# A Mamba scan on one core: the C rows stay in SBUF and only their changing half is refilled

## The chip, the core and the metric

The kernel runs on one core of a Trainium2 chip. A core has five engines that work side by side: TensorE (PE; PEld is its weight load), VectorE (DVE), ScalarE (ACT), GpSimd (POOL) and SyncE (SP), which here only issues DMAs. SBUF is the on-chip memory with 128 partitions, PSUM the matmul accumulator, and transfers are carried out by 16 DMA engines. The metric is the device time of one execution in microseconds (us).

## The reference

The input is x, [2, 96, 128, 128]. Layer 0 adds to x a four-direction Mamba over its normalised value, and then a quantised feed-forward; layer 1 adds a 3x3 convolution and a second feed-forward. The time lies in the Mamba. Each image has L = 16384 tokens, read in four orders: by rows, by rows backwards, by columns, by columns backwards. For each order (`xs4`, one set of weights each), with 192 channels d and 16 states s:

```python
xz = x @ in_w.T;  xc, z = jnp.split(xz, 2, axis=-1)
xc = jax.nn.silu(causal_conv4(xc) + conv_b)
xdbl = xc @ xproj_w.T                  # dt_raw (6), Bm (16), Cm (16) for each token
dt = jax.nn.softplus(dt_raw @ dt_w.T + dt_b)
def step(h, t):
    dA = jnp.exp(dt_t[:, :, None] * A)
    h = dA * h + dt_t[:, :, None] * B_t[:, None, :] * u_t[:, :, None]
    y = jnp.einsum('bds,bs->bd', h, C_t)
y = (ys + Dp * xc) * jax.nn.silu(z);   return y @ outp_w.T
```

B and C depend on the token and the state, not on the channel. So every channel (a partition of SBUF) needs the same row of B and of C, but each order has its own rows.

## The kernel before

For each of the two images there are three stages: `normalize` (layer norm, and a copy by columns to DRAM), `mamba`, and `ffn_and_conv`.

In `mamba` the two orders of a pair, rows and columns, go together: 2 x 192 channels fill three groups g of 128 partitions. Group 0 is the first order alone, group 2 the second alone, and group 1, the middle one, has the last 64 channels of the first and the first 64 of the second. A step is one pair and one stretch of T = 512 tokens; there are 2 pairs x 32 stretches for each image, 128 steps in all. Within a step the work goes over 24 units: the three groups, and in each the 16 states two by two (`units`, `nu`). Two units that follow one another are a quad of four states; a step has 12 quads.

For each unit ACT makes the decays `exp(dt * A)` into PSUM (`decay`), DVE runs two scans over 512 tokens (`scan`, L353), the state sequence h is multiplied with C (`behind`, L441, on DVE; in the six units of `BY_POOL` by POOL, L360), and PE adds the product into y by a matmul with the identity (`sums`, L357). Once in a quad POOL multiplies B with dt*u (`b_part`, L339), two units before the quad is scanned. When a group ends, DVE multiplies y with the gate (`gated`, L364) and PE projects it.

The rows of B and C come out of a matmul (`rows`), go to a DRAM tile `bcd` in the layout [B or C, quad, order, state, token], and are read back spread over 128 partitions by `row_tile` (L335): one 1 MB load for the B of a quad, into one of four buffers, and one for its C, into one of three. For groups 0 and 2 the source is one row of 8 KB repeated 128 times. For the middle group it is two rows, and the partitions alternate: even ones belong to the first order, odd ones to the second. The host lays the weights out in that order (`perm` in `_layout`). The middle group's conv and gate values come out of their matmul in halves (partitions 0 to 63 and 64 to 127), and are brought into the alternating order by DMAs (`mixed`, `mix`, L256).

The order of the work is written out by hand: each engine runs its instructions in program order (`in_order`), and `later`/`issue` put the next step's preparation (`prologue`) at given units. In iteration k of the main loop the calls are: the fetch of a B quad (k even), `feed` (POOL's multiplication for the quad after), the first scan of unit k, `behind(k - 1)` (product and sums of the unit before), the decays of unit k + 2, the second scan, the fetch of a C quad. A POOL product is issued at the end of the iteration after its unit's scans, and its sums two iterations later. All loads stand in SP's queue in this order, and a load waits there until the last reader of its buffer's former content is done.

Of the kernel before, what the change touches and what calls it, by code (L numbers as in the profile page):

```python
# [10 lines left out]
F32 = mybir.dt.float32  # L11
# [3 lines left out]
AF = mybir.ActivationFunctionType  # L15
ALU = mybir.AluOpType
# [13 lines left out]
HID = 384  # L30
PAIRS = ((0, 2), (1, 3))
NG = 3
B_AHEAD = 3
C_AHEAD = 2
AHEAD = 2
BY_POOL = tuple((g, s) for g in range(3) for s in (0, 8))
BCO = 32
NBC = 4 * S

# [2 lines left out]
def tile_metaformer(ctx: ExitStack, tc: tile.TileContext, a: dict, out: bass.AP):  # L42
# [142 lines left out]
    def mamba(acc, xnr, xnc):  # L185

        with ExitStack() as st:
            pool = lambda n, bufs, **kw: st.enter_context(tc.tile_pool(name=n, bufs=bufs, **kw))

            io, gen, one, mixp, two = (pool(*p) for p in (("io", 2), ("gen", 4), ("one", 1), ("mixp", 1), ("two", 2)))  # L190
# [23 lines left out]
            def prologue(pi, i, d):  # L214
# [34 lines left out]
                def mixed(name):  # L249
                    d["mix", name] = mixp.tile([128, T], F32, name="mix")  # L250
                    return d["mix", name]

                def mix(name):
# [51 lines left out]


                first = pi == 0 and i == 0
                at = [(-3, 1, load), (3, 0, partial(mix, "xc")), (11, 0, partial(silu, "xc"))]
                at += [(9, 0, partial(mix, "sz")), (31, 1, partial(silu, "sz"))]
# [28 lines left out]
            def b_part(i, d, g, s, b):  # L338
                nc.gpsimd.tensor_tensor(b, d["dtu"][g][:, None, :].broadcast_to((128, 4, T)), b, ALU.mult)  # L339
# [17 lines left out]
                    nc.tensor.matmul(y, ident, c[:, j, :], start=False, stop=s + j == S - 1)  # L357
# [32 lines left out]
            def later(k, where, rank, f, *args):  # L390
                todo.setdefault((k, where), []).append((rank, partial(f, *args)))
# [20 lines left out]
            prepare(1)  # L412
            bs, cs, das, hs, quads = {}, {}, {}, {}, {}

            def fetch(k, n, ahead, m):
                if k < total:
                    t = row_tile(state[k // nu], *units[k % nu], n, ahead)
                    m[k], m[k + 1] = t[:, 0:2, :], t[:, 2:4, :]
                    if n == 0:
                        quads[k] = t  # L420

            def feed(k):

# [11 lines left out]
            def behind(k):  # L435

                n, u = divmod(k, nu)
                (pi, i), d, (g, s) = steps[n], state[n], units[u]
                h, c = hs.pop(k), cs.pop(k)
                if (g, s) not in BY_POOL:  # L440
                    nc.vector.tensor_tensor(c, h, c, ALU.mult)  # L441
                nc.scalar.copy(hst[:, g, s : s + 2], h[:, :, T - 1])  # L442
                if s == 0:
                    if k > 0:
                        pn, pu = divmod(k - 1, nu)
                        gated(steps[pn][0], state[pn], units[pu][0], ys.pop(k - 1))
                    y = ps_y.tile([128, T], F32, name="y")
                    nc.tensor.matmul(y, dmat[:, pi, g, :], d["xc"][:, g, :], start=True, stop=False)  # L448
                else:
                    y = ys.pop(k - 1)  # L450
                ys[k] = y
                if (g, s) in BY_POOL:
                    later(k + 1, 1, True, by_pool, h, c)
                    later(k + 3, 1, True, sums, s, y, c)
                else:
                    sums(s, y, c)
# [6 lines left out]
            for m, (n, ahead) in ((bs, (0, B_AHEAD)), (cs, (1, C_AHEAD))):  # L463
                for k in range(ahead):
                    fetch(2 * k, n, ahead, m)
            feed(0)
            for k in range(AHEAD):
                feed_decay(k)
            for k in range(total + 6):
                n, u = divmod(k, nu)  # L470
                if u == nu - 3:

                    prepare(n + 2)
                if k % 2 == 0:
                    fetch(k + 2 * B_AHEAD, 0, B_AHEAD, bs)
                    feed(k + AHEAD)
                issue(k, 0)
                if k < total:
                    (g, s) = units[u]
                    da, b = das.pop(k), bs.pop(k)  # L480
                    hs[k] = b if (g, s) in BY_POOL else da
# [118 lines left out]
def _layout(v):  # L600

    f = np.float32
    order = [d for pair in PAIRS for d in pair]

    perm = np.arange(2 * DI)
    perm[128:256] = perm[128:256].reshape(2, 64).T.reshape(-1)
    grouped = lambda w: w.reshape(2, NG, 128, -1).transpose(2, 0, 1, 3)
    plain = lambda w: grouped(w[order].reshape(2, 2 * DI, -1))
    rows = lambda w: grouped(w[order].reshape(2, 2 * DI, -1)[:, perm])
# [19 lines left out]
    out = {  # L629
        "x": v["x"].reshape(NB, C, L),  # L630
        "ident": np.eye(128, dtype=f),
        "inx": v["L0_conv_in_w"][:, :DI].transpose(2, 0, 1),
        "inz": v["L0_conv_in_w"][:, DI:].transpose(2, 0, 1),
        "taps": v["L0_conv_conv_w"].transpose(0, 2, 1)[None],
        "convb": plain(v["L0_conv_conv_b"])[..., 0],
        "bcw": grouped(bcw[:, perm]),
        "dtw": dtw[:, :, perm],
        "dtb": rows(v["L0_conv_dt_b"])[..., 0],
        "alog": rows(v["L0_conv_A_log"]),
        "dskip": rows(v["L0_conv_Dp"])[..., 0],  # L640
        "outx": outx,
        "fusew": v["L0_conv_fuse_w"].reshape(C, 4, C).transpose(2, 1, 0),
        "fuseb": v["L0_conv_fuse_b"].reshape(C, 1),
        "kw": v["L1_conv_kernel"].transpose(1, 2, 3, 0).reshape(C, 9, C),
    }
# [23 lines left out]
```

## Time and profile before

| | us |
|---|---|
| median of 3 runs | 11550.38 (11546.19 to 11551.36) |
| profiled execution | 11556.77, its span 11555.0 |
| DVE busy | 10421.6 (90%) |
| PE busy | 10435.0 (90%) |
| POOL busy | 9672.3 (84%) |
| ACT busy | 7901.7 (68%) |
| DMA traffic | 3417 MB, 296 GB/s over the span |
| granted TensorE clock | 0.989 |

The two scan stages run from about 120 to 5200 us and from about 5900 to 10980 us. In the page's slices they are where DVE, PE and POOL show nines and the DMA engines eights; between and after them stand `ffn_and_conv` and `normalize`, with hardly any transfers. In a group's line the numbers after the bar are the busy time, the mean of one instruction in ns, and the idle time of the engine just before such an instruction with what ended most of it. In a line of waits they are the total in us, how often, and the longest.

### The profile page before, as it was taken

The page shows a single profiled execution, that of the slowest core. Times are in us where ns is not written, and L with a number is a line of the kernel's source. Part 1 is how long each engine was busy: PE and PEld are TensorE (multiplying, and loading weights), DVE is VectorE, ACT ScalarE, POOL GpSimd, SP SyncE. Part 2 cuts the span into 40 slices and gives each one's busy share as a digit, 9 for nine tenths or more (in the row PEclk, how much of TensorE's full clock was granted, in tenths as well). Part 3 has the DMA queues.
Part 4 walks back from the last instruction along what each step waited for, and adds up shares of the span by engine and source line. Part 5 has one row for each costly group of instructions (what it writes and reads, how often), then busy time and mean ns, then how long its engine had stood idle before and what let it go on. Part 6 is the DMA issues. An engine that isn't in the chain of part 4 may idle for free. (4 is left out here: it accounts for less than half of the span.)

```text
span 11555.0 us, 94102 instructions
## 1 busy us (share of the span) xinstructions
PE 10435.0 (90%) x24208; PEld 3971.4 (34%) x24208; DVE 10421.6 (90%) x10127; ACT 7901.7 (68%) x13564; POOL 9672.3 (84%) x4700
## 2 busy tenths in 40 slices
PE   7999999999999999989989999999999999999899
PEld 2333333333333333333323333333333333333333
DVE  6999999999999999994469999999999999999944
ACT  6767767677677677665567677677676776776655
POOL 5999999999999999991159999999999999999911
PEclk8999999999999999999989999999999999999999
DMA  7888888888888888880068888888888888888800
GB/s 263 335 329 333 333 332 332 330 331 333 329 332 333 330 331 333 329 322 19 26 243 334 328 331 334 330 333 333 333 331 329 332 332 329 331 333 329 319 13 13
DMA packets 540755, 3416.96 MB, mean 296 GB/s; under 512 B 67532, under 2 KB 68652, under 8 KB 143832
## 3 DMA queue, kind: packets, MB, share of 16 engines
q1 hardware_dynamic: 539960, 3410.16, 76.8%
q8 instruction: 196, 3.21, 0.1%
q14 instruction: 343, 2.81, 0.1%
q0 software_dynamic: 256, 0.79, 0.0%
HBM read 3289.04 MB, written 54.53 MB: 289 GB/s over the span
## 5 line engine op out<-in xcount | busy, mean ns | idle before, releaser
L339 POOL TENSOR_TENSOR row<-dtu,row 128x2048 f32<-128x2048 f32 x1536 | 6948.9, 4524 | 283.3 <-DMA row<-bcd 281.6
L357 PE MATMUL y<-row,ident 128*128 128x512 f32 x12288 | 5690.6, 603 | 700.0 <-DVE row L441 699.9
L353 DVE TENSOR_TENSOR_SCAN da<-da,row 128x512 f32<-128x512 f32 x4608 | 5456.9, 1214 | 38.9 <-ACT da L349 5.2
L349 ACT ACTIVATE da<-dt,amat 128x512 f32<-128x512 f32 x6144 | 4246.9, 691 | 170.2
L357 PEld LDWEIGHTS y<-row,ident 128*128 128x128 f32 x12288 | 2256.8, 190 | 4008.4 <-issue 2243.5
L441 DVE TENSOR_TENSOR row<-da,row 128x1024 f32<-128x1024 f32 x2304 | 2776.7, 1205 | 70.2 <-DMA row<-bcd 70.0
L442 ACT COPY hst<-da 128x2 f32<-128x2 f32 x2304 | 368.9, 160 | 2652.2 <-DVE row L441 2649.3
L360 POOL TENSOR_TENSOR row<-row,row 128x1024 f32<-128x1024 f32 x768 | 1807.4, 2353 | 223.0 <-DVE row L353 147.5
L353 DVE TENSOR_TENSOR_SCAN row<-da,row 128x512 f32<-128x512 f32 x1536 | 1852.4, 1206 | 91.9 <-POOL row L339 84.1
L211 PE MATMUL misc<-xa,inx 96*64 96x512 f32 (+1 forms) x2048 | 946.1, 605 | 50.0 <-ACT mix L239 26.8
L211 PE MATMUL misc<-xb,inx 96*64 96x512 f32 (+1 forms) x2048 | 952.3, 608 | 33.6 <-ACT hst L442 24.2
L564 POOL TENSOR_TENSOR acc<-acc,y 96x512 f32<-96x512 f32 x128 | 147.4, 1151 | 991.5 <-DVE y L563 991.5
L298 POOL TENSOR_TENSOR dtu<-dt,xc 128x512 f32<-128x512 f32 x384 | 487.4, 1269 | 106.0 <-DMA xb<-xnc 99.8
L576 PE MATMUL pc<-pad,kw 96*96 96x512 f32 x1152 | 566.4, 593 | 0.0
L211 PEld LDWEIGHTS misc<-xa,inx 96*64 96x64 f32 (+1 forms) x2048 | 327.3, 165 | 581.2 <-issue 438.0
L448 PE MATMUL y<-xc,dmat 128*128 128x512 f32 x768 | 419.5, 628 | 103.6 <-DVE sz L364 103.6
L374 PE MATMUL misc<-sz,gmat 128*96 128x512 f32 x1024 | 484.1, 595 | 0.0
L284 PE MATMUL misc<-rows,dtw 12*128 12x512 f32 x768 | 434.3, 645 | 50.6 <-ACT dt L289 37.9
L364 DVE TENSOR_TENSOR sz<-y,sz 128x512 f32<-128x512 f32 x384 | 264.6, 689 | 229.5 <-PE y L357 198.0
L136 DVE TENSOR_TENSOR xq<-xm,rs 96x512 fp8e5<-96x512 f32 x128 | 87.9, 687 | 392.2 <-ACT rs L132 392.2
L211 PEld LDWEIGHTS misc<-xb,inx 96*64 96x64 f32 (+1 forms) x2048 | 316.5, 164 | 361.9 <-issue 214.1
L372 PE MATMUL misc<-acc,ident 96*96 96x512 f32 x512 | 387.6, 842 | 57.3 <-ACT sz L247 53.8
(76 smaller groups left out, 7449.9 us busy)
## 6 DMA issues: line engine op xcount, KB each, us to landing
row<-bcd SPq DMA_DIRECT2D x3072, 1024.0 KB, 7.4
xc<-mix SPq DMA_DIRECT2D x256, 128.0 KB, 5.4
sz<-mix SPq DMA_DIRECT2D x256, 128.0 KB, 8.9
xa<-xnr SPq DMA_DIRECT2D x124, 193.1 KB, 8.6
xb<-xnc SPq DMA_DIRECT2D x124, 193.1 KB, 8.7
bcd<-rows SPq DMA_DIRECT2D x128, 128.0 KB, 9.5
acc<-in_x_dram SPq DMA_DIRECT2D x16, 768.0 KB, 5.7
xnr<-xn SPq DMA_DIRECT2D x16, 768.0 KB, 4.3
```

The source lines that it names most:

```text
L211: nc.tensor.matmul(ps[rows, :], w(PAIRS[pi][d], k, lo, hi), src[d][:, k : k + T], **se)
L284: nc.tensor.matmul(d["ps"], w, d["rows"][0 : 2 * RK, :], start=True, stop=True)
L298: nc.gpsimd.tensor_tensor(dtu, d["dt"][:, g, :], d["xc"][:, g, :], ALU.mult)
L339: nc.gpsimd.tensor_tensor(b, d["dtu"][g][:, None, :].broadcast_to((128, 4, T)), b, ALU.mult)
L349: nc.scalar.activation(da[:, j, :], d["dt"][:, g, :], AF.Exp, scale=amat[:, pi, g, s + j : s + j + 1])
L353: nc.vector.tensor_tensor_scan(h[:, j, :], da[:, j, :], b[:, j, :], 0.0, ALU.mult, ALU.add)
L357: nc.tensor.matmul(y, ident, c[:, j, :], start=False, stop=s + j == S - 1)
L360: nc.gpsimd.tensor_tensor(c, h, c, ALU.mult)
L374: nc.tensor.matmul(d["po"], gmat[:, pi, 2 * g - 2 + k, :], d["yg"][g - 1 + k], start=False, stop=k == 1)
L441: nc.vector.tensor_tensor(c, h, c, ALU.mult)
L448: nc.tensor.matmul(y, dmat[:, pi, g, :], d["xc"][:, g, :], start=True, stop=False)
L576: nc.tensor.matmul(pc, kw[:, t, :], rows, start=t == 0, stop=t == 8)
```

## The change

- The C rows are no longer loaded for each quad into rotating buffers. Four tiles `crow0` to `crow3`, one for each quad of states, stay for the whole stage. `c_fill` refills one of them when the products of its quad are done: from group 0 to group 1 only partitions 64 to 127 change their order of tokens, from group 1 to group 2 only partitions 0 to 63, and from group 2 to the next step's group 0 all 128.
- The middle group is in halves: partitions 0 to 63 belong to the first order, 64 to 127 to the second. So `perm`, `mixed` and `mix` go, and the source of the middle group's B load is written as two rows, each repeated 64 times (`src[:, None].broadcast_to((n, 128 // n, 4, T))`), where it was 64 repeats of two rows.
- The products with C are written into the unit's B buffer instead of the C buffer. There are five B buffers in place of four, `B_AHEAD` is 4 in place of 3, and the fetch stands after the second scan of the iteration, with the C fill behind it.
- POOL's products are those of the states s = 2 and 8 in each group, in place of 0 and 8.
- The program's scratch for DMAs issued by POOL is 4096 bytes.

```diff
-B_AHEAD = 3
-C_AHEAD = 2
+B_AHEAD = 4
-BY_POOL = tuple((g, s) for g in range(3) for s in (0, 8))
+BY_POOL = tuple((g, s) for g in range(3) for s in (2, 8))
...
-                    t = mixed("xc") if g == 1 else d["xc"][:, g, :]
-                    nc.scalar.activation(t, d["ps"], AF.Identity, bias=convb[:, pi, g : g + 1])
+                    nc.scalar.activation(d["xc"][:, g, :], d["ps"], AF.Identity, bias=convb[:, pi, g : g + 1])
...
-                    nc.scalar.copy(mixed("sz") if g == 1 else d["sz"][:, g, :], d["ps"])
+                    nc.scalar.copy(d["sz"][:, g, :], d["ps"])
...
-                    for k in range(2):
-                        nc.sync.dma_start(d[name][k:128:2, 1, :], d["mix", name][64 * k : 64 * k + 64, :])
...
-            def row_tile(d, g, s, k, ahead):
-                t = gen.tile([128, 4, T], F32, name=f"row{k}", bufs=ahead + 1)
-                src = d["bcd"][k, s // 4] if g == 1 else d["bcd"][k, s // 4, g // 2 : g // 2 + 1]
+            def row_tile(d, g, s):
+                t = gen.tile([128, 4, T], F32, name="row", bufs=B_AHEAD + 1)
+                src = d["bcd"][0, s // 4] if g == 1 else d["bcd"][0, s // 4, g // 2 : g // 2 + 1]
                 n = src.shape[0]
-                nc.sync.dma_start(t, src[None].broadcast_to((128 // n, n, 4, T)))
+                nc.sync.dma_start(t, src[:, None].broadcast_to((n, 128 // n, 4, T)))
                 return t
+            crow = [one.tile([128, 4, T], F32, name=f"crow{q}") for q in range(S // 4)]
+            def c_fill(n, g, q):
+                if n < len(steps):
+                    part = (slice(0, 128), slice(64, 128), slice(0, 64))[g]
+                    src = state[n]["bcd"][1, q, int(g > 0)]
+                    nc.sync.dma_start(crow[q][part], src[None].broadcast_to((part.stop - part.start, 4, T)))
...
-                nc.gpsimd.tensor_tensor(c, h, c, ALU.mult)
+                nc.gpsimd.tensor_tensor(h, h, c, ALU.mult)
...
-                h, c = hs.pop(k), cs.pop(k)
+                h, b, c = hs.pop(k), cs.pop(k), crow[s // 4][:, s % 4 : s % 4 + 2, :]
                 if (g, s) not in BY_POOL:
-                    nc.vector.tensor_tensor(c, h, c, ALU.mult)
+                    nc.vector.tensor_tensor(b, h, c, ALU.mult)
...
                 if k % 2 == 0:
-                    fetch(k + 2 * B_AHEAD, 0, B_AHEAD, bs)
                     feed(k + AHEAD)
...
                 if k % 2 == 0:
-                    fetch(k + 2 * C_AHEAD, 1, C_AHEAD, cs)
+                    fetch(k + 2 * B_AHEAD)
+                    if 4 <= k < total + 4:
+                        cn, cu = divmod(k - 4, nu)
+                        cg, cq = cu // 8, cu % 8 // 2
+                        c_fill(cn + (cg == 2), (cg + 1) % 3, cq)
...
-        outx[:, pi, 1, 0::2] = ow[p, :, 128:]
-        outx[:, pi, 2, 1::2] = ow[q, :, :64]
+        outx[:, pi, 1, :64] = ow[p, :, 128:]
+        outx[:, pi, 2, 64:] = ow[q, :, :64]
...
-        "dtw": dtw[:, :, perm],
+        "dtw": dtw,
...
-    nc = bacc.Bacc("TRN2", target_bir_lowering=False, num_devices=1)
+    nc = bacc.Bacc("TRN2", target_bir_lowering=False, num_devices=1, dynamic_dma_scratch_size=4096)
```

More of the change, by code (lines that the diff above doesn't have):

```diff
@@ L188, in mamba @@
             pool = lambda n, bufs, **kw: st.enter_context(tc.tile_pool(name=n, bufs=bufs, **kw))
-            io, gen, one, mixp, two = (pool(*p) for p in (("io", 2), ("gen", 4), ("one", 1), ("mixp", 1), ("two", 2)))
+            io, gen, one, two = (pool(*p) for p in (("io", 2), ("gen", 4), ("one", 1), ("two", 2)))
             ps_w, ps_y, ps_m = (pool(n, k, space=PSUM) for n, k in (("ps_w", 3), ("ps_y", 1), ("ps_m", 1)))
@@ L246, in gate_out @@
                         d["sz"] = two.tile([128, NG, T], F32, name="sz")
-                    nc.scalar.copy(mixed("sz") if g == 1 else d["sz"][:, g, :], d["ps"])
[L249 to L253, printed above, removed]
-                    for k in range(2):
-                        nc.sync.dma_start(d[name][k:128:2, 1, :], d["mix", name][64 * k : 64 * k + 64, :])
+                    nc.scalar.copy(d["sz"][:, g, :], d["ps"])
                 def silu(name):
@@ L307, in prologue @@
                 first = pi == 0 and i == 0
-                at = [(-3, 1, load), (3, 0, partial(mix, "xc")), (11, 0, partial(silu, "xc"))]
-                at += [(9, 0, partial(mix, "sz")), (31, 1, partial(silu, "sz"))]
+                at = [(-3, 1, load), (11, 0, partial(silu, "xc"))]
+                at += [(31, 1, partial(silu, "sz"))]
                 at += [(12, 0, rows), (13, 1, rows_out), (14, 0, rows_to_dram)]
@@ L413, in mamba, with fetch @@
             bs, cs, das, hs, quads = {}, {}, {}, {}, {}
-            def fetch(k, n, ahead, m):
+            def fetch(k):
                 if k < total:
[L417 to L420, printed above, removed]
+                    quads[k] = t = row_tile(state[k // nu], *units[k % nu])
+                    bs[k], bs[k + 1] = t[:, 0:2, :], t[:, 2:4, :]
             def feed(k):
@@ L452, in behind @@
                 if (g, s) in BY_POOL:
-                    later(k + 1, 1, True, by_pool, h, c)
-                    later(k + 3, 1, True, sums, s, y, c)
+                    later(k + 1, 1, True, by_pool, b, c)
+                    later(k + 3, 1, True, sums, s, y, b)
                 else:
-                    sums(s, y, c)
+                    sums(s, y, b)
                 if k == total - 1:
@@ L461, in behind @@
                     later(k + 5, 1, False, collect, pi, d, g)
-            for m, (n, ahead) in ((bs, (0, B_AHEAD)), (cs, (1, C_AHEAD))):
-                for k in range(ahead):
-                    fetch(2 * k, n, ahead, m)
+            for k in range(B_AHEAD):
+                fetch(2 * k)
+                c_fill(0, 0, k)
             feed(0)
@@ L480, in mamba @@
                     da, b = das.pop(k), bs.pop(k)
+                    cs[k] = b
                     hs[k] = b if (g, s) in BY_POOL else da
@@ L603, in _layout @@
     order = [d for pair in PAIRS for d in pair]
-    perm = np.arange(2 * DI)
-    perm[128:256] = perm[128:256].reshape(2, 64).T.reshape(-1)
     grouped = lambda w: w.reshape(2, NG, 128, -1).transpose(2, 0, 1, 3)
     plain = lambda w: grouped(w[order].reshape(2, 2 * DI, -1))
-    rows = lambda w: grouped(w[order].reshape(2, 2 * DI, -1)[:, perm])
     xw = v["L0_conv_xproj_w"]
@@ L635, in _layout @@
         "convb": plain(v["L0_conv_conv_b"])[..., 0],
-        "bcw": grouped(bcw[:, perm]),
-        "dtw": dtw[:, :, perm],
-        "dtb": rows(v["L0_conv_dt_b"])[..., 0],
-        "alog": rows(v["L0_conv_A_log"]),
-        "dskip": rows(v["L0_conv_Dp"])[..., 0],
+        "bcw": grouped(bcw),
+        "dtw": dtw,
+        "dtb": plain(v["L0_conv_dt_b"])[..., 0],
+        "alog": plain(v["L0_conv_A_log"]),
+        "dskip": plain(v["L0_conv_Dp"])[..., 0],
         "outx": outx,
```

## The prediction

> **What bounds the kernel now.** I read the page's head and slices, then the stretches, the groups, the waits and the DMA issues.
>
> ```profile
> span 11555.0 us, 94102 instructions
> ...
> PE 10435.0 (90%) x24208; PEld 3971.4 (34%) x24208; DVE 10421.6 (90%) x10127; ACT 7901.7 (68%) x13564; POOL 9672.3 (84%) x4700
> ...
> DVE  6999999999999999994469999999999999999944
> ...
> DMA  7888888888888888880068888888888888888800
> ```
> ```profile
> 2000.00:3000.00 1000.00, 909.25 (x2095) 344.99 (x2094) 967.53 (x873) 704.02 (x1211) 937.99 (x444) 1.00 0.86 332
> ```
> The columns of the stretch are PE, PEld, DVE, ACT, POOL, granted clock, DMA share, GB/s. In the two scan stages DVE is busy 967 of 1000 us and sets the pace; the 16 DMA engines are busy 86% of the time and still mostly hidden, as the waits say:
> ```profile
> POOL row L339 <- DMA row<-bcd: 281.6, 307, 3.6
> ...
> DVE sz L364 <- PE y L357: 198.0, 207, 3.1
> ...
> DVE row L441 <- DMA row<-bcd: 70.0, 121, 1.3
> ```
> DVE waited for the C rows (L441) 70 us in all, 0.6% of the span. One step of the loop (24 units, 12 quads) can be read off the chain, which names the same piece at the same place of each step:
> ```profile
> 8996.39 5.42 PE y L357 x12
> 9075.49 5.42 PE y L357 x12
> 9154.78 5.42 PE y L357 x12
> ```
> So a step takes 79.1 us and a quad 6.59; there are 2 x 2 x 32 = 128 steps, 10,125 us. The prices inside a quad:
> ```profile
> L339 POOL TENSOR_TENSOR row<-dtu,row 128x2048 f32<-128x2048 f32 x1536 | 6948.9, 4524 | 283.3 <-DMA row<-bcd 281.6
> ...
> L353 DVE TENSOR_TENSOR_SCAN da<-da,row 128x512 f32<-128x512 f32 x4608 | 5456.9, 1214 | 38.9 <-ACT da L349 5.2
> ...
> L441 DVE TENSOR_TENSOR row<-da,row 128x1024 f32<-128x1024 f32 x2304 | 2776.7, 1205 | 70.2 <-DMA row<-bcd 70.0
> ```
> and the transfers:
> ```profile
> q1 hardware_dynamic: 539960, 3410.16, 76.8%
> ```
> ```profile
> row<-bcd SPq DMA_DIRECT2D x3072, 1024.0 KB, 7.4
> ...
> dtw<-in_dtw_dram SPq DMA_DIRECT2D x1, 36.0 KB
> ```
> Each row load is 128 packets of 8 KB. In the trace's transfer records such a packet takes 0.311 us (median of 396,637; least 0.307), and 16 or 17 packets are open in 80% of a scan stretch: one per engine, 8 per engine and load, 8 x 0.311 = 2.5 us.
>
> **The change, part by part.**
>
> *Less traffic.* Per step 12 B and 12 C loads of 1 MB become 12 B loads, 4 full C fills and 8 half fills: 20 MB for 24. The four mix DMAs of a step go too. This can return at most what DVE lost to C rows, 70 us. Of the waits on mix, DVE had 13 us (L364): zero.
>
> *Compute.* The products have the same count and shapes (18 by DVE, 6 by POOL in a step), now into b instead of c: 1205 and 2353 ns as before, zero. POOL's unit s=2 in place of s=0 moves a product, its sums and the gate by one unit: zero, bounded by the 198 us of L364 either way. The smaller scratch concerns the four loads on POOL's queue: zero.
>
> *Longer hold on b.* A buffer is now free only after the sums. A fetch stands behind the scan of the quad four ahead, so it goes out about 1.2 (scan) + 1.2 (product) + 2.0 (four sum passes) = 4.4 us into that quad; for the POOL units s=2 a quad later. With five buffers a load has still 9.7 us before POOL wants it (issue at 16.7 us, wanted at 26.4), against 7.4 to land: zero if loads keep their price. Queued behind that wait on SP are the next C fill, the next fetch and bcd.
>
> *The middle group's B load.* Here the price changes. Before, its source was walked as 64 repeats of 2 rows; now `src[:, None]` makes it 2 rows of 64 repeats, so its outermost count is 2. What does the split over engines follow? The nearest row is dtw, 12 rows: its completion semaphore shows one write at once and then 12 landings, while the transfers of 64, 96 and 128 rows show 16. The number of engines followed the outer count there. Two rows would then use two engines: 64 packets each, 64 x 0.311 = 19.9 us in place of 2.5. The bounds are 2.5 (16 engines as today) and 39.8 (all on one); I take two engines, since dtw is the only row with an outer count under 16. With the mean under load (76.8% of 16 engines for 11,555 us over 3,410 MB, 43.7 engine-us per 1 MiB) it would be 21.8.
>
> [...]
>
> *What the 19.9 us does.* I take it that all four loads use the same two engines (rival C prices the other case). With one packet open per engine, everything on these two stands in line, the C fills too, whose shares on them are behind the B loads issued ahead of them. A full fill costs 2.5 us. A half fill is 4 packets per engine: 1.2 at the usual price, 2.5 if it is no quicker than a full one; the 8 KB packets of the 96-row loads at the program's start take 0.512 in the median, so I take 2.0. Set the start of a step's quad 0 to 0. SP's order is: fetch g1 quad 0, C for g0 quad 2 (full); fetch g1 quad 1, C for g0 quad 3 (full); fetch g1 quad 2, C for g1 quad 0 (half); fetch g1 quad 3, C for g1 quad 1 (half). The first goes out at 4.4, and a load's least time to land, 4.1, is 1.6 over its 2.5, so about 1.0 to its first packet and 0.6 after its last. The fetches are out before the two engines are free (the second at 16.7, the fourth about 3 us after C for g0 quad 3 lands). The chain:
> 4.4 + 1.0 + 4 x 19.9 + 2 x 2.5 + 2 x 2.0 + 0.6 = 94.6 us.
> Then the last fill has landed and the first product of g1 quad 1 can run. DVE is in order, so this product holds the next scan: 1.2 + 1.2 later, at 97.0, quad 6 starts. The other six quads (fetches of 2.5 us again) run at 6.59: 39.5. The step takes 136.5 in place of 79.1, +57.4. Along the way DVE would stand at C for g0 quad 2 (lands near 28, wanted at 21), for g0 quad 3 (near 51), for g1 quad 0 (73) and quad 1 (95).
>
> 128 x 57.4 = 7,347. On the profiled execution's 11,556.8 (span 11,555.0; 6.4 above the median 11,550.4, 0.06%, and so no matter here) this gives 18,904: **18,900 us**. DVE, PE and POOL fall to 51 to 55% busy (their old busy time over the new span), and the mean DMA rate to roughly 2,815 MB / 18.9 ms = 150 GB/s.
>
> With 21.8 per load the step is 144.1: 19,880. With half fills at 1.2 it is 134.9: 18,700.
>
> [...]
>
> **The rivals.**
> *A, the load is split over 16 engines after all* (not slower). Then each load stays at 2.5 us and only the waits for C rows go: 11,557 - 70 = 11,487, with the late fetches and slow half fills 11,430 to 11,620. For it: every 128-partition destination in this trace landed 16 times. Against it: none of these had an outer count under 16. It decides from here: C for g1 quad 1 is wanted at 37.5 on the old pace, and 5.4 + 4d + 9 + 0.6 is within that up to d = 5.6 us, so eight engines (5.0) would do, four (9.9) not.
> *B, deeper overlap.* If fetching ahead hid the chain, only the sum on the two engines would count: 4 x 19.9 + 8 x 2.5 + 4 x 2.5 + 8 x 2.0 + 1.3 (xa, xb, bcd) = 126.9 a step: 17,680; with half fills at 1.2, 120.5: 16,860. Against it: the fetch distance is four quads, so the first slow load cannot go out before quad 0.
> *C, the four loads take different pairs of engines.* Then they overlap and each fill waits for one load only: C for g0 quad 3 lands at 40.7, the fourth load goes out at 44.5 and its fill lands at 68, quad 6 starts at 70.4, the step takes 109.9: 15,500. The trace has no row that says which engines a 12-row load took.
>
> **How the numbers follow.** The forecast 80%, A 11%, B 5%, C 4%. A load priced between 19.6 (64 x 0.307) and 21.8 us and B lie in 16,800 to 19,950; some 4% of the forecast may lie above it (a packet slower when 64 follow on one engine). Outside remain A, C and that: a little under 2 in 10. A measurement here tells 0.2% (23 us) from no change. Slower: forecast, B, C and a quarter of A, 0.92; of A the rest is faster 0.06, same 0.02.
>
> **What would show it.** Right: the B issues of the middle group take about 20 us or more to land (the median of all can stay near 8); DVE's wait at the product for a DMA grows from 70 to some thousands of us; of each step some 79 us run at the old pace and some 57 stand; bytes fall to some 2.8 GB. Wrong: 16 landings at the usual spacing and a DMA rate near 245 GB/s (A); stalls of one load length only (C). A longer wait of POOL at L335 of the new kernel instead of DVE's would mean that the B rows themselves, not the C fills behind them, come last.

## The result and the profile after

The changed kernel takes 21,721.25 us (median of 4, 21,708.91 to 21,726.28) against 11,550.87 before: ratio 1.8804, 95% interval 1.8771 to 1.8836. It is slower, as forecast, but 2,820 us above the forecast and above the end of its range (19,950). The profiled execution's span is 21,720.0 us.

The page's head, slices and queues:

```profile
span 21720.0 us, 91178 instructions
...
PE 11959.8 (55%) x24208; PEld 4505.1 (21%) x24208; DVE 10526.6 (48%) x10127; ACT 7961.0 (37%) x13564; POOL 9682.9 (45%) x4700
...
DVE  4545445454454544545445454454544545444444
...
DMA  4434434343443434433044344343443434334330
...
q1 hardware_dynamic: 426296, 2806.11, 38.8%
```

The work is the same: DVE and POOL are busy as long as before (10,526.6 and 9,682.9 us against 10,421.6 and 9,672.3), over nearly twice the span. PE's 1,525 us more go with the granted clock, 0.762 in the mean for 0.989: the clock is low where PE is kept waiting (0.57 from 4126 to 4151 us, where PE is busy 5.3 of 25 us; 0.91 from 4200 to 4250, busy 37.7 of 50). Fewer bytes move (2,806 MB on SP's queue for 3,410), and the 16 engines are busy 39% for 77%. So none of the core's engines is at its limit, nor are the 16 DMA engines taken together; the time is waiting. The stretch of 1000 us whose fellow was shown of before (columns PE, PEld, DVE, ACT, POOL, granted clock, DMA share, GB/s) has DVE busy 475 us for 968 and 133 GB/s for 332:

```profile
3000.00:4000.00 1000.00, 517.97 (x1021) 194.94 (x1021) 474.55 (x423) 348.18 (x590) 459.05 (x222) 0.75 0.40 133
```

The groups and the waits (total in us, times, longest) name what is waited for:

```profile
L336 POOL TENSOR_TENSOR row<-dtu,row 128x2048 f32<-128x2048 f32 x1536 | 6931.5, 4513 | 6606.9 <-DMA row<-bcd 6585.8
L436 DVE TENSOR_TENSOR row<-da,crow 128x1024 f32<-128x1024 f32 x2304 | 2791.9, 1212 | 10046.6 <-DMA crow<-bcd 10045.3
```
```profile
DVE row L436 <- DMA crow<-bcd: 10045.3, 893, 38.3
...
POOL row L357 <- DMA crow<-bcd: 2272.5, 126, 19.9
```

One product took 1212 ns, as before (1205); what grew is the wait in front of it, from 70 us to 10,045, for the C fills. Those 9,975 us are 98% of the 10,165 by which the span grew. (The longer span over 128 steps gives 79.4 us more for each step: 158.5 in place of 79.1.) The chain says the same: 45% of the span is the transfer of `crow`, 11% that of B rows.

In DVE's timeline (start, duration, in brackets the idle time before), one step has four long waits for a fill:

```profile
4126.64 1.23 DVE L436 TENSOR_TENSOR row<-da,crow 128x1024 f32<-128x1024 f32 x1 [14.05 <-DMA crow<-bcd]
...
4151.00 1.22 DVE L436 TENSOR_TENSOR row<-da,crow 128x1024 f32<-128x1024 f32 x1 [20.89 <-DMA crow<-bcd]
...
4174.04 1.22 DVE L436 TENSOR_TENSOR row<-da,crow 128x1024 f32<-128x1024 f32 x1 [16.21 <-DMA crow<-bcd]
...
4200.22 1.22 DVE L436 TENSOR_TENSOR row<-da,crow 128x1024 f32<-128x1024 f32 x1 [19.72 <-DMA crow<-bcd]
```

They stand at the products with C for g0 quad 2, g0 quad 3, g1 quad 0 and g1 quad 1: the four places that the prediction named. Together they are 70.9 us of this step. In SP's queue of the same step, three issues in themselves take 10 to 20 us, where 0.5 to 0.6 is usual (the run's medians are 0.48 for a B load and 0.61 for a fill):

```profile
4095.88 0.48 SPq L323 DMA_DIRECT2D row<-bcd  x1
4096.40 0.59 SPq L333 DMA_DIRECT2D crow<-bcd  x1
4097.56 0.55 SPq L323 DMA_DIRECT2D row<-bcd  x1
4098.15 0.59 SPq L333 DMA_DIRECT2D crow<-bcd  x1
4110.82 0.53 SPq L323 DMA_DIRECT2D row<-bcd  x1
4111.40 12.03 SPq L333 DMA_DIRECT2D crow<-bcd  x1
4123.55 2.09 SPq L323 DMA_DIRECT2D row<-bcd  x1
4125.68 20.35 SPq L333 DMA_DIRECT2D crow<-bcd  x1
4158.24 0.51 SPq L323 DMA_DIRECT2D row<-bcd  x1
4158.79 10.18 SPq L333 DMA_DIRECT2D crow<-bcd  x1
```

The issues at 4097.56, 4110.82, 4123.55 and 4158.24 are the four loads of the middle group, and behind each stands its C fill. In the transfer records, exactly two packets are open for half of the time from 3000 to 3500 us. A middle group's load is 64 packets in line on each of two engines, 64 x 0.313 = 20.0 us, and its semaphore shows one write at once and then two landings. Of the 16 landings of the fill issued at 4111.40, 14 come from 4127.40 to 4128.42, and the last two at 4149.52 and 4150.90, behind the load of 4110.82 (4146.16 and 4147.26).

### The profile page after: what moved, and what is told of

Same layout as the page of the kernel before. It is cut to its first block, busy times and chain, and to the rows that moved or that the text cites. A ratio compares the mean times of both kernels' runs of the same rounds, so it can differ in the third digit from the quotient of the medians.

```text
span 21720.0 us, 91178 instructions
## 1 busy us (share of the span) xinstructions
PE 11959.8 (55%) x24208; PEld 4505.1 (21%) x24208; DVE 10526.6 (48%) x10127; ACT 7961.0 (37%) x13564; POOL 9682.9 (45%) x4700
## 4 chain that ended last, share of the span: by engine, by line
DMA 56%; PE 27%; POOL 7%; issue 4%; DVE 3%; ACT 1%; SPq 1%; another core or an unknown queue 1%; POOLq 0%; DVEq 0%; ACTq 0%
DMA crow<-bcd 45%; PE y L354 15%; DMA row<-bcd 11%; POOL row L336 5%; PE pc L575 2%; DVE row L436 2%; PE misc L210 2%; PE misc L255 2%; POOL row L357 1%; PE misc L371 1%; PE misc L369 1%; PE xm L121 1%; PE v L127 1%; SPq L323 1%; POOL dtu L287 1%
## 5 line engine op out<-in xcount | busy, mean ns | idle before, releaser
L354 PE MATMUL y<-row,ident 128*128 128x512 f32 x12288 | 7019.3, 720 | 7436.8 <-DVE row L436 6758.9
L436 DVE TENSOR_TENSOR row<-da,crow 128x1024 f32<-128x1024 f32 x2304 | 2791.9, 1212 | 10046.6 <-DMA crow<-bcd 10045.3
L354 PEld LDWEIGHTS y<-row,ident 128*128 128x128 f32 x12288 | 2726.3, 230 | 11541.7 <-issue 8124.3
L357 POOL TENSOR_TENSOR row<-row,crow 128x1024 f32<-128x1024 f32 x768 | 1807.5, 2353 | 4087.8 <-DMA crow<-bcd 2272.5
L350 DVE TENSOR_TENSOR_SCAN row<-da,row 128x512 f32<-128x512 f32 x1536 | 1851.6, 1205 | 0.0
L443 PE MATMUL y<-xc,dmat 128*128 128x512 f32 x768 | 553.7, 810 | 1902.3 <-DVE sz L361 1902.3
L210 PE MATMUL misc<-xa,inx 96*64 96x512 f32 (+1 forms) x2048 | 939.1, 601 | 27.8 <-DMA xa<-xnr 17.5
L443 PEld LDWEIGHTS y<-xc,dmat 128*128 128x128 f32 x768 | 140.2, 229 | 2218.4 <-DVE sz L361 2116.1
L255 PE MATMUL misc<-xc,bcw 128*96 128x512 f32 x768 | 435.5, 711 | 7.1 <-ACT xc L248 7.1
```

Source lines behind the costliest of these rows:

```text
L210: nc.tensor.matmul(ps[rows, :], w(PAIRS[pi][d], k, lo, hi), src[d][:, k : k + T], **se)
L255: nc.tensor.matmul(d["ps"][0 : BCO + NBC, :], bcw[:, pi, g, :], d["xc"][:, g, :], start=g == 0, stop=g == NG - 1)
L350: nc.vector.tensor_tensor_scan(h[:, j, :], da[:, j, :], b[:, j, :], 0.0, ALU.mult, ALU.add)
L357: nc.gpsimd.tensor_tensor(h, h, c, ALU.mult)
L436: nc.vector.tensor_tensor(b, h, c, ALU.mult)
```

## The experiments

My theory: the order in which the middle group's B load is written confines it to two engines, the C fills stand behind it on those two, and everything else in the change is near zero. The rivals of the runs below: the load does not matter (the held buffers or the half fills do), or the rest of the change has a price of its own. A time without an interval is that of a single run.

### The source order alone, in both directions

Run e1: the changed kernel, the middle B load cut into two loads, one row each.

```diff
-                src = d["bcd"][0, s // 4] if g == 1 else d["bcd"][0, s // 4, g // 2 : g // 2 + 1]
-                n = src.shape[0]
-                nc.sync.dma_start(t, src[:, None].broadcast_to((n, 128 // n, 4, T)))
+                for a in range(2) if g == 1 else (g // 2,):
+                    part = slice(64 * a, 64 * a + 64) if g == 1 else slice(0, 128)
+                    src = d["bcd"][0, s // 4, a]
+                    nc.sync.dma_start(t[part], src[None].broadcast_to((part.stop - part.start, 4, T)))
```

> The changed kernel, with the middle group's B load cut into two loads of 64 partitions, each from one row, so that the outermost count is 64. Theory (the outermost count of 2 puts the load on two engines, and that is the whole loss): both halves use 16 engines, 4 packets each at 0.31 to 0.64 us, 2.5 to 5 us for the pair; the step is back at about 79 us, 11,430 to 11,650 us in all, DVE's wait for C rows under 150 us. Rival (the new scheme itself costs: B buffers held longer, C tiles with one buffer each and filled behind the B loads): at least 3 us a step stay, 11,950 us or more, with SP or DVE waiting at the same places.

Run e4: the kernel before, with only the order of its middle B load as in the change (its even and odd partitions then hold other rows of B than its weights are laid out for).

```diff
-                nc.sync.dma_start(t, src[None].broadcast_to((128 // n, n, 4, T)))
+                if k == 0:
+                    nc.sync.dma_start(t, src[:, None].broadcast_to((n, 128 // n, 4, T)))
+                else:
+                    nc.sync.dma_start(t, src[None].broadcast_to((128 // n, n, 4, T)))
```

> The kernel before with one thing changed: the middle group's B load walks its two rows as 2 rows of 64 repeats. (The partitions then hold the other order's B row in half of the middle group, so this part of the computation is changed; the work is the same.) Theory: this alone makes most of the loss: four loads of 20 us a step on two engines, C loads behind them in SP's line, and a fetch distance of three quads; by the same chain a step of 133 us and, with what the changed kernel's trace showed beyond the chain, up to 155: 18,500 to 21,300 us. Rival (the loss needs the single C tiles and the longer hold): under 13,000 us.

e1 took 13,712.39 us (ratio 1.1865, 1.1845 to 1.1885), e4 21,154. So the order of one source makes nearly the whole loss alone (e4 is 9,603 us above before), and taking it out returns 8,009 of 10,170. e4 lies at the upper end of its expectation, which the changed kernel's trace had set: the chain of the prediction alone gave 133 us a step there, and a step took 154.1. But e1 missed its expectation of 11,430 to 11,650 by 2,000: something else in the change costs that much. Its waits name two things above all, POOL's product waiting for ACT's copy and DVE for the C fills:

```profile
POOL row L358 <- ACT hst L438: 2030.4, 615, 7.9
DVE row L437 <- DMA crow<-bcd: 2016.9, 750, 8.2
...
POOL row L337 <- DMA row<-bcd: 562.0, 426, 4.6
```

### The dose: eight and four engines

Runs e2 and e3: e1 with each half's 64 repeats written as 8 x 8 and 4 x 16 (the diff shows the line that matters in e2; `dst` is the same half of the tile, `t[part]` in e1).

```diff
-                    nc.sync.dma_start(t[part], src[None].broadcast_to((part.stop - part.start, 4, T)))
+                        nc.sync.dma_start(dst, src[None, None].broadcast_to((8, 8, 4, T)))
```

> As e1_halves, but each half's source is written as 8 repeats of 8 repeats, so that the outermost count is 8; bytes, partitions and packets are the same. Theory: 8 engines, 8 packets each, two halves make 16 x 0.311 = 5.0 us a load on them. The chain as it was worked out beforehand (5.4 + 4 x 5.0 + 9 + 0.6 = 35, wanted at 37.5) gives no loss: about 11,500 us. With the terms as the changed kernel's trace shows them (first slow load 12.6 us into the step, fills 10 us) quad 6 starts at about 45 instead of 39.6: about 12,300 us. Rival (the engine count does not follow the outermost count): the same time as e1_halves.

> As e2_eight with an outermost count of 4: 4 engines, 32 packets each for the two halves, 10.0 us a load. By the chain as worked out beforehand quad 6 starts at 57.4 and the step takes 96.9: 13,830 us. With the terms that the changed kernel's trace shows (start 12.6, pairs of load and fill up to 2 us longer, 46 us for the last six quads) 115 us a step: 16,150 us. Rival (the count does not matter): as e1_halves.

Outermost counts of 64, 8, 4 and 2 gave 13,712, 15,906, 17,938 and 21,721 us (the last is the changed kernel, with one load in place of two halves). The time rises with each step down. The engines can be counted in the transfer records from 3000 to 3500 us: exactly eight packets are open for 22% of the time in e2, exactly four for 30% in e3, exactly two for 50% in the changed kernel. Both e2 and e3 lie above what was expected: the prediction had let eight engines pass free, and they cost 2,194 us over e1, whose own unexplained 2,000 us they carry too.

### What else costs: order, POOL's units, the place of s=2

All of these change e1 (e5, e6, e8) or the changed kernel (e7, e11). e5 and e7 put the C fill ahead of the fetch; e6 and e11 give POOL's six units to DVE; e8 puts s=2 back to s=0.

```diff
                 if k % 2 == 0:
-                    fetch(k + 2 * B_AHEAD)
                     if 4 <= k < total + 4:
...
                         c_fill(cn + (cg == 2), (cg + 1) % 3, cq)
+                    fetch(k + 2 * B_AHEAD)
```
```diff
-BY_POOL = tuple((g, s) for g in range(3) for s in (2, 8))
+BY_POOL = ()
```

> e1_halves with one line moved: in each iteration the C fill is issued before the B fetch instead of behind it. e1_halves stands at 96 us a step against 79, and DVE waits 2017 us for C rows. Theory H (hold): a B fetch waits in SP's queue until POOL's product and its sums have freed the buffer, and the C fill behind it goes out with the next one, some 13 us late; moved ahead of it, the fill is no longer held: DVE's wait for C falls under 300 us and the time to 11,450 to 11,900 us. Theory P (half transfers are slow in themselves, their 8 KB packets take 0.64 us): the waits for C stay, 13,000 us or more.

> e1_halves with all products on DVE, none on POOL, so that no buffer is held for POOL. Theory H: the waits for C go (under 300 us) although DVE has six products more in a step, 6 x 1.21 = 7.3 us; the step is DVE's work, 79.1 + 7.3 = 86.4 us, 12,300 to 12,800 us in all, faster than e1_halves. Theory P: the waits stay and DVE's work comes on top in part, 13,700 us or more.

> e1_halves with POOL's products at the states s = 0 and 8, as in the kernel before, instead of 2 and 8. Theory H: the unit s = 0 is the first of its quad, so its buffer is held a unit (3.3 us) less than with s = 2; half of the held fetches gain that much: the step 3 to 8 us less, 12,700 to 13,350 us. Theory P: no change, 13,700 us.

e5 took 12,046.9 (ratio 1.0427, 1.0404 to 1.0449), e6 12,147, e8 13,055; e8 held its expectation, e6 did better and e5 came 147 us above the end of its own. Each returns a large part of e1's loss: 1,665, 1,565 and 657 us. e6 is the telling one: DVE has six products more in each step (7.3 us, 930 in all) and the kernel is still much faster. The reason can be read in e1's SP queue:

```profile
4034.40 0.33 SPq L324 DMA_DIRECT2D row<-bcd  x1
4034.77 0.63 SPq L334 DMA_DIRECT2D crow<-bcd  x1
4036.12 0.33 SPq L324 DMA_DIRECT2D row<-bcd  x1
4036.49 0.45 SPq L334 DMA_DIRECT2D crow<-bcd  x1
...
4051.46 0.33 SPq L324 DMA_DIRECT2D row<-bcd  x1
4051.84 0.45 SPq L334 DMA_DIRECT2D crow<-bcd  x1
4054.38 0.33 SPq L324 DMA_DIRECT2D row<-bcd  x1
4054.75 0.44 SPq L334 DMA_DIRECT2D crow<-bcd  x1
```

A fetch held until POOL's product and its sums are done holds the C fill behind it too, although the fill's own tile is free. Then two fetches and two fills go out within 2 to 4 us, followed by some 15 us with no such load. The fills come late, DVE stands, and with DVE the copy for which POOL's product waits. With the fill ahead of the fetch, DVE's wait for fills fell from 2,017 to 211.5 us (e5):

```profile
DVE row L437 <- DMA crow<-bcd: 211.5, 205, 5.1
...
POOL row L337 <- DMA row<-bcd: 868.6, 540, 6.2
```

What e5 may come up against then are the transfers, although fewer bytes move than before: their share is 0.93 at 257 GB/s.

```profile
3000.00:4000.00 1000.00, 886.92 (x1980) 342.50 (x1979) 921.06 (x823) 666.80 (x1145) 886.26 (x429) 0.97 0.93 257
```

The same two edits on the changed kernel itself:

> The changed kernel with the C fill issued before the B fetch, B loads on two engines as they are. If the fills stand in line behind the slow loads: a fill is now behind one slow load less, the wait for the last C fill of the middle group moves to the wait for the last slow load, one quad later, and the late start of a step's first slow load is partly cured: 8 to 13 us a step less, 20,000 to 20,700 us, and POOL's wait for B rows grows while DVE's for C shrinks. If the fills are not in that line: 21,700 us as before.

> The changed kernel, with its B loads on two engines, and all products on DVE, so that no buffer is held for POOL. If the hold is what the forecast's chain left out: the first slow load starts near 5 us instead of 12.6, the last six quads run at DVE's pace again (39.5 + 6 x 0.6 = 43 instead of 46.4), the pairs of load and fill stay as measured (96.6 instead of 88.6): 5.4 + 96.6 + 2.4 + 43 = 147.5 us a step, 20,300 us; with the pairs as forecast 139.5: 19,280. If the hold plays no part: DVE's additional work is hidden in the waits, 21,700 us or more.

e7 took 20,877, e11 20,645: 844 and 1,076 us less, both within 350 us of what was expected. With the slow load in place the order of the two matters less, and most of the wait only moves: in e7 DVE's wait for fills falls from 10,045 to 5,910 and POOL's for B rows rises from 6,586 to 9,428.

### Half fills to alternate partitions

Run e9: C tiles as in the change, fill ahead of the fetch, but the middle group alternates as in the kernel before (with `mix`, the host's order and the 64 repeats of two rows), and a half fill goes to every second partition. The loads that POOL's queue issued go to SP, with a smaller scratch. Run e10 is e9 with the fetch first, e12 is e9 with s=0 for s=2.

```diff
-                    part = (slice(0, 128), slice(64, 128), slice(0, 64))[g]
+                    part = (slice(0, 128), slice(1, 128, 2), slice(0, 128, 2))[g]
```

> The C tiles stay and the C fill goes ahead of the B fetch, as in e5_halves_c_first, but the middle group's partitions alternate between the two orders as in the kernel before: its B load is one transfer of 64 repeats of two rows, the half C fills write 64 alternate partitions, and the mix copies are back (with them the POOL queue's four loads go to SP, and its scratch is 2048 bytes). In e5 the DMA engines were busy 91 to 93% of the time at 257 GB/s, and 8 KB packets of half transfers took 0.63 to 0.66 us. Theory (64 neighbouring partitions take twice as long, alternate ones do not): packets at 0.31, DMA share about 70%, POOL's wait for B rows (869 us in e5) under 300 us, 11,430 to 11,620 us. Rival (any 64-partition transfer is slow, or the held fetch is what is left): 11,900 us or more.

> e9_alternate with the C fill behind the B fetch, as in the changed kernel. Theory H (hold): the fills are late by the held fetch whatever the layout; DVE's wait for C rows is 500 us or more, the step 4 to 14 us longer than in e9: 12,000 to 13,300 us. If instead slow half transfers made the fills late: as e9_alternate.

> e9_alternate with POOL's products at s = 0 and 8 as in the kernel before. Theory H: the hold of the first quad is a unit shorter; with the C fills ahead of the fetches this matters to B loads alone, which have 8 us against some 5 to land: 0 to 150 us less than e9_alternate.

e9 took 11,887.91 (ratio 1.0289, 1.0274 to 1.0304), 159 us less than e5. The transfers are no longer the limit: the share fell from 0.93 to 0.71 while the rate rose to 274 GB/s, POOL waits 26.9 us for B rows (868.6 in e5), and DVE 0.1 us for fills (211.5).

```profile
3000.00:4000.00 1000.00, 904.37 (x2056) 348.72 (x2054) 948.71 (x851) 685.58 (x1180) 916.67 (x446) 0.98 0.71 274
```

In the transfer records from 3000 to 3500 us a packet of 8 KB took 0.326 us in the median and 0.627 in the upper quartile in e1, and 0.309 and 0.318 in e9. Four in ten of these packets belong to half transfers in e1, two in ten in e9, where nine in ten packets took 0.378 or less. So the slow packets went with the neighbouring halves: in e5, which has them and the fill ahead of the fetch as e9 does, the packets of half transfers took 0.63 to 0.66 us. Yet e9 stayed 337 us above before, a miss against 11,430 to 11,620, and its longest new wait was one that no transfer causes:

```profile
POOL row L366 <- ACT hst L446: 815.6, 258, 5.8
```

e10 took 12,407, as expected, 519 us more than e9: the fetch ahead of the fill costs with alternate halves too (DVE waits 787.2 us for fills). e12 took 11,980.96 (ratio 1.0374, 1.0357 to 1.0392), 93 more than e9 where I had expected less.

### The parts of POOL's share, one by one

Run e13 removes e9's wait: POOL copies the last column for its own units, before its product. e16 is e13 with s=0 for s=2.

```diff
-            def by_pool(h, c):
+            def by_pool(h, c, last):
+                nc.gpsimd.tensor_copy(last, h[:, :, T - 1])
                 nc.gpsimd.tensor_tensor(h, h, c, ALU.mult)
...
-                nc.scalar.copy(hst[:, g, s : s + 2], h[:, :, T - 1])
+                if (g, s) not in BY_POOL:
+                    nc.scalar.copy(hst[:, g, s : s + 2], h[:, :, T - 1])
```

> e9_alternate has lost its waits for transfers (DVE 0.1 us for C, POOL 27 us for B) and is still 330 us above the kernel before; POOL's product waits 816 us for ScalarE, which copies the last state out of h before the product may overwrite it there. Here POOL makes that small copy itself, right before its product, for its own units; nothing else changes. If the in-place product behind ScalarE's copy is what is left: POOL's wait for ScalarE goes, 11,480 to 11,650 us. If the rest comes from the place of the POOL units, or from PE and ScalarE work that falls together: 11,800 us or more.

> The version of run e13 (C tiles stay, C fill first, alternate partitions in the middle group, POOL makes the copy of the last column for its own units) with POOL's units back at s=0 and 8. Theory 1, the unit s=2 still costs in e13: ACT's copy of the gate waited 412 us for PE there (107 in the kernel before, 495 in e14 where s=2 is the only change) and DVE then 195 us for ACT's decay. With s=0 both go: 11,480 to 11,600. Theory 2, once the C tiles stay, s=0 is no better than s=2 because its product follows the fills of quad 0 directly, as in e12 against e9 (+93 us): 11,700 to 11,850.

The other two take one part of the change each into the kernel before: e14 only `s in (2, 8)`, e15 only the product written over h in the B buffer.

```diff
-BY_POOL = tuple((g, s) for g in range(3) for s in (0, 8))
+BY_POOL = tuple((g, s) for g in range(3) for s in (2, 8))
```
```diff
-                nc.gpsimd.tensor_tensor(c, h, c, ALU.mult)
+                nc.gpsimd.tensor_tensor(h, h, c, ALU.mult)
...
-                    later(k + 3, 1, True, sums, s, y, c)
+                    later(k + 3, 1, True, sums, s, y, h)
```

> The kernel before with POOL's products at s = 2 and 8 instead of 0 and 8. The forecast took this part as zero: 11,530 to 11,580 us. If the place of these units is what keeps e9_alternate slow: 11,700 us or more.

> The kernel before with POOL's products written in place over h, in the B buffer, as in the changed kernel, instead of into the C buffer; DVE's products stay in the C buffers. This is the hold on b and the wait for ScalarE's copy alone, with four B buffers and a fetch distance of three quads. If these two cost time by themselves: POOL waits for ScalarE 500 us or more and for B rows several hundred us more than the 282 of before, 11,750 to 12,800 us. If they are hidden, as the forecast had it: 11,550 to 11,600 us.

e14 took 12,093.08 (ratio 1.0468, 1.0452 to 1.0484), e15 11,545.05 (0.9996, 0.9987 to 1.0006). So POOL's product in place is free, and the unit's place alone costs 544 us. The waits in SP's queue show where the loads are held. Of the kernel before:

```profile
SPq L335 <- PE y L357: 6879.4, 1404, 11.1
...
SPq L335 <- POOL row L360: 114.7, 171, 3.2
```

and of e14:

```profile
SPq L335 <- PE y L357: 4676.0, 1403, 9.7
SPq L335 <- POOL row L360: 1797.3, 510, 7.9
SPq L335 <- ACT hst L442: 1259.7, 382, 14.6
```

With POOL's product one unit later in the quad, the buffers of that quad come free later, and the next loads stand in SP's queue behind that. Once issued, a load takes no longer to land than before (7.3 us in the median, 7.4 before). The rows come late to POOL and to DVE's products, and by POOL to DVE's scans:

```profile
POOL row L339 <- DMA row<-bcd: 843.3, 423, 4.8
```
```profile
DVE row L441 <- DMA row<-bcd: 411.3, 200, 4.5
...
DVE da L353 <- POOL row L343: 345.8, 258, 2.4
```

The first was 281.6 before, the second 70.0, and the third was not among the seven longest waits of DVE (under 62 us).

e13 took 11,701.71 (ratio 1.0133, 1.0116 to 1.0149), 52 us above its expectation, and the nearest to the kernel before of all versions that keep the C tiles; 151 us are left. e16 was to show whether the place of s=2 is what is left. It took 12,040.22 (median of 5, 11,989 to 12,069; ratio 1.0429, 1.0414 to 1.0443), so theory 1 of its expectation falls, and the range of theory 2 (to 11,850) is missed too. ACT's wait for PE at the gate's copy did go (412.5 to 99.0 us), but DVE still waited 185.8 us for the decay (194.8 in e13), and DVE's own multiplication with the gate waited 559.9 us for the last sums (78.6 in e13). With fixed C tiles s=0 is the worse place when the partitions alternate, by 339 us; in e1, with neighbouring halves and the fetch ahead of the fill, it is the better one by 657. What the last 151 us of e13 are made of stays open.

No version that keeps the C tiles beat the kernel before, and of the single parts tried in it only the product in place did no harm.

## Why the prediction was wrong in size

*The split over two engines: right.* It was the term that carried the forecast. Two packets open, 20.0 us for a load (19.9 was taken), two landings, and e4 with the source's order alone at 21,154. Rival A (16 engines) fell.

*All four on the same two engines, fills in line behind the loads, the first product of each quad waiting: right.* The four waits stand where they were put, and from 4129 to 4145 us, with two of the loads under way, exactly two packets are open for 98% of the time. Rival C (other pairs) would have had one load length for each wait and 15,500; rival B (deeper overlap) 17,680. Both fell.

*The chain of a step: right in kind, some 22 us too short.* The step shown starts at 4090.0 (the first scan of its quad 0), the next at 4249.4: 159.4 us in place of 136.5. The table takes it apart at points that DVE's timeline shows, with the means over 121 of the 128 steps (those at the ends of the two stages left out), and the same of e11, which has no POOL units:

| us | forecast | this step | mean | mean in e11 |
|---|---|---|---|---|
| start of the step to the end of the first wait | 28.4 | 36.6 | 36.1 | 31.9 |
| from there to the end of the fourth wait (three slow loads, each with its fill) | 66.2 | 73.6 | 72.0 | 75.3 |
| to the start of quad 6 | 2.4 | 2.3 | 2.3 | 2.3 |
| the six quads after | 39.5 | 46.9 | 48.7 | 41.0 |
| step | 136.5 | 159.4 | 159.0 | 150.5 |

So three terms were mis-sized, by 7.7, 5.8 and 9.2 us in the mean. Times 128 that is 2,880 us, for the 2,820 that were missing.

The failed step, as far as the runs show it, is *"Longer hold on b"*, put at zero, and with it POOL's unit "s=2 in place of s=0", put at zero and bounded by the 198 us of L364. The text priced the hold as lead time of one load (9.7 us against 7.4 to land). It listed what is queued behind the held fetch on SP, "the next C fill, the next fetch and bcd", and gave that no price. The runs did:

- The fill behind a held fetch: 1,665 us (e1 to e5) and 519 us (e9 to e10).
- s=2 by itself: 544 us in the kernel before (e14); the bound of 198 came from a wait on DVE, but the loads are held on SP. Its sign depends on the rest: with alternate partitions s=0 was the worse place (e12, e16). In the changed kernel itself no run put it back.
- All of POOL's units together: 1,565 us in e1, though DVE then does more, and 1,076 in the changed kernel (e11).
- POOL's product in place: zero, as taken (e15). No run took DVE's products into the B buffer by themselves.

In the changed kernel this shows at both ends of the chain. The first slow load goes out 7.6 us after the start of the step (4097.56), where the forecast had 4.4, and only 1.7 us behind the fetch ahead of it, which is held by POOL's s=8 unit of the group before. That fetch and its fill are then in line ahead of it. After the stall the last six quads take 7.8 us each instead of 6.59. Without POOL's units both ends nearly go: in e11 a step starts at 4038.0, the first slow load goes out 4.4 us later, as forecast, with the fetch ahead of it 6.7 us in front, and DVE stands nowhere in the six quads after the stall.

```profile
4035.71 0.48 SPq L323 DMA_DIRECT2D row<-bcd  x1
...
4042.44 0.55 SPq L323 DMA_DIRECT2D row<-bcd  x1
```

The first term falls by 4.2 us and the last by 7.7; the middle one grows by 3.3, and 8.5 of the 22.5 us are returned. e11 takes away POOL's product, its wait for ACT's copy (1,815 us in the changed kernel) and the held fetches together, so that the hold is the cause within them is argued from SP's queue.

The middle term, 24.0 us for each load and fill in place of 22.1, stays open. In this step the second of the two engines lands 0.5, 1.1, 2.1 and 2.8 us after the first in the four loads, and a fill needs both. It is not the hold alone: e4, with neither the C tiles nor the longer hold nor s=2, has a step 21 us longer than the same chain gave for it (154.1 for 133). There POOL waits for the slow rows themselves (9,760 us) more than DVE for C (3,973), so its excess cannot be set against the three terms one by one.

*Less traffic returns at most 70 us*: no run shows that it returned anything. *A half fill at 2.0 us*: with neighbouring partitions half the bytes took as long as the whole: 4 packets of 0.627 us (the upper quartile in e1) are 2.5 us, as are 8 of 0.311. The bytes (2,815 MB forecast, 2,812.7 measured) were right, and the saving in transfer time that they suggest was not there.

*Rival A's point of decision, d up to 5.6 us, so that eight engines would do: wrong.* Eight engines cost 2,194 us. The point was worked out from one chain of fills, with everything else of the change at zero, and e1 shows that it was not zero; what the eight engines add to that was not taken apart.

*The range.* It was made from the price of the load alone, 19.6 to 21.8 us, and all else at zero on both sides. A bound for the hold from the trace was at hand: each step has six POOL units, and one fetch held by half a quad in each would add 6 x 3.3 = 20 us to a step, 2,530 us in all. On top of 19,950 that end would have held the result.

## What to carry to other kernels

Before a transfer is reordered, read the outermost count of its access pattern: here 2 x 64 instead of 64 x 2 took a load from 16 engines to two (an estimated 2.5 us of packets to 20.0) and everything behind it with it. When a buffer is held longer, price what stands behind the held load in the same queue, not only the load's own lead time, and issue first what is free to go. And before a saving in bytes is counted as a saving in time, read how long the smaller transfer's packets take: here, with half transfers to every second partition, the upper quartile was 0.318 us (e9), with neighbouring halves 0.627 (e1).

## What the runs showed of the hardware

- An issue on SP's queue is not always short. In the changed kernel, with two loads of 64 packets per engine under way, SP stood 12.0, 20.4 and 10.2 us in the issue of a fill in the step shown (27.8 at most in the run), until 0.1, 0.1 and 0.7 us before the first of the older load's two landings. The median issue of a fill there is 0.61 us, of a B load 0.48, of a row load in the kernel before 0.37.
- With half transfers to 64 neighbouring partitions the upper quartile of the 8 KB packets was 0.627 us (e1), twice that with half transfers to 64 alternate partitions (0.318, e9).
- The number of engines in use went with the outermost count: with 8, 4 and 2, exactly eight, four and two packets were open for 22, 30 and 50% of the time from 3000 to 3500 us (e2, e3, the changed kernel), and the time rose at each: 15,906, 17,938 and 21,721 us, for 13,712 with 64 (e1).
- PE's granted clock followed its waiting: in four stretches of the stall (4102 to 4125, 4126 to 4151, 4155 to 4174 and 4177 to 4200 us) it was 0.87, 0.57, 0.77 and 0.57, with PE busy 60, 21, 44 and 18%; 0.91 in the 50 us after it (75%), 1.00 in the stretch of the kernel before (91%).
